# Block kernel (window attention, then FFT filter and convolution), last strips: VectorE's order written out by the plan, the last 1x1 convolution of an older strip between a strip's two transforms, and GpSimd's first tap as a product of its own

## The chip, the cores and the metric

One core of one Trainium2 chip. The metric is the device time of one execution in microseconds, the median of several runs. The core has five engines with queues of their own, each in order: TensorE (PE; its weight loads are shown as PEld), VectorE (DVE), ScalarE (ACT), GpSimd (POOL) and SyncE (SP), which here issues DMAs.

## The reference

Two layers over x of shape (8, 384, 64, 64) in float32. Layer 0 is a window attention. Layer 1, the one that the change touches, is, cut to what matters:

```python
def _L1_conv_ref(x, fft_filter, w_in, w_dw, w_out):
    t = jnp.einsum('bchw,oc->bohw', x, w_in)              # 1x1 convolution in
    tp = t.reshape(b, hid, hb, P, wb, P)                  # 8x8 blocks
    tf = jnp.fft.rfft2(tp, axes=(3, 5))
    tf = tf * fft_filter[None, :, None, :, None, :]
    t = jnp.fft.irfft2(tf, s=(P, P), axes=(3, 5)).reshape(b, hid, h, w)
    t = jax.lax.conv_general_dilated(t, w_dw, ...)        # 3x3, each channel by itself
    x1, x2 = (t[:, :hid // 2], t[:, hid // 2:])
    g = jax.nn.gelu(x1, approximate=False) * x2
    return jnp.einsum('bchw,oc->bohw', g, w_out)          # 1x1 convolution out

x = x + _L0_conv_ref(_gn(x), ...)
x = x + _L1_conv_ref(_gn(x), ...)
```

`_gn` normalises each group of 12 channels over a whole image, so layer 1 of an image starts only when layer 0 of that image is complete.

## The kernel before

An image is 8 strips of 8 rows (512 positions), 384 channels in three planes of 128 partitions. (b,s) stands for strip s of image b below. Layer 1 of image b runs beside layer 0 of image b+1; behind the last image's layer 0 there is only its own layer 1, strip after strip. All instructions are put out by a plan: `at(place, piece, ...)` notes a piece with a place, a number in which one unit is half a strip, and the pieces are traced in the order of their places. TensorE's matmuls are pinned to that order (`keep_in_program_order`, called `in_order` too). On the other engines a scheduler orders the instructions at build time by its own estimate of when each is ready, with the plan's order as priority; a pinned instruction stays behind the one traced before it on its engine.

The pieces of a strip (b,s) of layer 1, with u = 16 (b+1) + 2 + 2 s, and the names by which the profile knows their tiles:

- `load` "mix" at u-0.84 (x_mix, on SP); `normal_x1` (xn, ScalarE, L652); `mix` four times from u+0.28 (pt on TensorE, copied by ScalarE to t1, L662).
- `transform` j = 0, 1 at u+0.995 and u+1.02: the forward transform pf on TensorE, and VectorE's product with the filter (t2, L679, two for each j; the profile calls the tiles t).
- `back` at u+1.99: the inverse transform pz on TensorE, then ScalarE's copies into z (L707), a plane of 10 x 66 with a border. `borders` copies the third plane and then the border rows between a strip and the one above it: L716 writes the lower border of the strip above, L717 the upper border of this one.
- the 3x3 convolution, nine taps for each of the planes m = 0, 2, 1 in the order of `TAPS`: the centre tap 0 by ScalarE (L777), the others by VectorE (`conv`, L783, a multiply-add). Taps 6, 7, 8 read the lower border row and need the next strip's pz.
- for the strips in `on_pool`, (6,7) and (7,0) to (7,6), plane 1 is done elsewhere (`pool_taps`): ScalarE multiplies a tap (L751, pairs of tiles in three buffers), GpSimd adds (L755 for taps 0 and 1 together, L759 for each other one). Their planes 0 and 2 add up in PSUM (tile acc); other strips add up in SBUF (tile zz).
- for (7,7), in `on_pe`, all of plane 1 and five taps of plane 2 are matmuls (`conv_taps`, pc).
- `gate` at u+4.5: gelu on ScalarE (L798 or L801, L802), two products of half height on VectorE (L803, L804), and the product of planes 0 and 1 (L805), on GpSimd for strips in `on_pool`.
- `load` "finish" at u+5.16, and `finish` at u+6.10: the convolution out, pw on TensorE (from g1 first, then from the product g0), the additions to x_finish on VectorE (L833, L835 or L839), the output DMA on SP.

A strip's `finish` therefore comes, two strips on, behind that strip's `back` and before the next one's `mix`. The tiles pt, pf, pw and pz share four buffers of PSUM (tag "gemm"); acc and pc share two pairs of banks (tag "att").

Of the kernel before, what the change touches and what calls it, by code (L numbers as in the profile page):

```python
# [12 lines left out]
P = 128  # L13
# [24 lines left out]
def block_kernel(ctx: ExitStack, tc: tile.TileContext, out, x, consts, fsel, wqk, wv, bqk, bv,  # L38
# [262 lines left out]
    def at(place, piece, *args):  # L301
        plan.append((place, len(plan), piece, args))
# [362 lines left out]
    def transform(b, s, j):  # L665

        pf_ = [psum(f"pf_{b}_{s}_{j}_{p}") for p in range(2)]
        t2 = zs[b, s, "t2", j] = sb.tile([P, 2, 2, C // 2], F32, tag="t2", bufs=3, name=f"t2_{b}_{s}_{j}")  # L670
        for i in range(2):
            t1 = zs.pop((b, s, "t1", 2 * j + i))
            for h in range(2):
                for p in ((0, 1), (1, 0))[h]:
                    rows, cols = slice(p * 64, (p + 1) * 64), slice(h * 64, (h + 1) * 64)
                    matmul(pf_[p][cols, i * 192:(i + 1) * 192], fwd[rows, rows],
                           t1[rows, h * 192:(h + 1) * 192], start=True, stop=True)
        for p in range(2):
            nc.vector.tensor_tensor(t2[:, p], pf_[p][:, 0:C].rearrange("p (i c) -> p i c", i=2),  # L679
                                    feff.unsqueeze(1).to_broadcast([P, 2, C // 2]), ALU.mult)  # L680

    def back(b, s):

# [34 lines left out]

    TAPS = (4, 0, 1, 2, 3, 5, 6, 7, 8)
    on_pe = {(B - 1, NS - 1): {2: 5, 1: 9}}
    on_pool = [(B - 2, NS - 1)] + [(B - 1, s) for s in range(NS - 1)]

    def tap_matrices():
# [16 lines left out]
    def pool_taps(b, s, taps):  # L742

        z = zs[b, s, 1]
        for j in range(0, len(taps), 2):
            tag = ("o", "e", "eT")[zs["pairs"] % 3]
            zs["pairs"] += 1
            pair = sb.tile([P, 2, ST], F32, tag=tag, bufs=1, name=f"tap_{b}_{s}_{taps[j]}")
            for i, tap in enumerate(taps[j:j + 2]):
                dy, dx = TAPS[tap] // 3, TAPS[tap] % 3  # L750
                nc.scalar.activation(pair[:, i].rearrange("p (r c) -> p r c", c=SW), z[:, dy:dy + 8, dx:dx + SW],  # L751
                                     AF.Copy, scale=dw_sb[:, 1, TAPS[tap]:TAPS[tap] + 1])
            if tap == 1:
                zz = zs[b, s, "zz", 1] = row512("qk", 5, f"zz_{b}_{s}_1")
                nc.gpsimd.tensor_tensor(zz, pair[:, 0], pair[:, 1], ALU.add)  # L755
            else:
                zz = zs[b, s, "zz", 1]
                for i in range(len(taps[j:j + 2])):
                    nc.gpsimd.tensor_tensor(zz, zz, pair[:, i], ALU.add)  # L759

    def conv(b, s, m, tap):

        if m == 1 and (b, s) in on_pool:
            return
        z = zs[b, s, m]
        n = on_pe.get((b, s), {}).get(m, 0)
        if tap < max(n, 1):
            return
        if tap == max(n, 1):
            if (b, s) in on_pool:  # L770
                if m == 0:
                    zs[b, s, "in psum"] = psum2(f"acc_{b}_{s}")
                zz = zs[b, s, "in psum"][:, m // 2]
            else:
                zz = row512("zz", 5, f"zz_{b}_{s}_{m}")
            if n == 0:
                after_out(nc.scalar.activation(zz.rearrange("p (r c) -> p r c", c=SW), z[:, 1:9, 1:SW + 1],  # L777
                                               AF.Copy, scale=dw_sb[:, m, 4:5]))
                zs[b, s, "zz", m] = zz
            zs[b, s, "acc", m] = zz  # L780
        acc, old = zs[b, s, "acc", m], zs[b, s, "zz", m]
        dy, dx = TAPS[tap] // 3, TAPS[tap] % 3
        i = nc.vector.scalar_tensor_tensor(acc.rearrange("p (r c) -> p r c", c=SW),  # L783
                                           z[:, dy:dy + 8, dx:dx + SW], dw_sb[:, m, TAPS[tap]:TAPS[tap] + 1],
                                           old.rearrange("p (r c) -> p r c", c=SW), ALU.mult, ALU.add)

        if b < B - 1 and m and tap == 1:
            tc.keep_in_program_order(i)
        if b < B - 1:
            after_softmax(i)  # L790
        zs[b, s, "zz", m] = acc

    def gate(b, s):
        zz = {m: zs[b, s, "zz", m] for m in range(KC)}
        g1 = row512("g1", 2, f"g1_{b}_{s}")
        if (b, s) in on_pool:
            whole = row512("zz", 5, f"zz_{b}_{s}_0")
            nc.scalar.activation(whole, zz[0], AF.Gelu)  # L798
            zz[0] = whole
        else:  # L800
            nc.scalar.activation(zz[0], zz[0], AF.Gelu)  # L801
        nc.scalar.activation(g1[64:P], zz[2][0:64], AF.Gelu)  # L802
        nc.vector.tensor_tensor(g1[0:64], g1[64:P], zz[2][64:P], ALU.mult)  # L803
        nc.vector.tensor_tensor(g1[64:P], g1[64:P], zz[2][64:P], ALU.mult)  # L804
        (nc.gpsimd if (b, s) in on_pool else nc.vector).tensor_tensor(zz[0], zz[0], zz[1], ALU.mult)  # L805
        zs[b, s, "g"] = zz[0], g1

    def finish(b, s):


        g0, g1 = zs[b, s, "g"]
        t = xs[b, s, "finish"]

        full, lo, hi = slice(0, ST), slice(0, 256), slice(256, ST)
        pw = [psum(f"pw_{b}_{s}_{m}") for m in range(3 if (b, s) in on_pool else 2)]
        if (b, s) in on_pool:
            pw = [(p, m, full) for m, p in enumerate(pw)]
        else:
            pw2 = psum2(f"pw2_{b}_{s}")
            pw = [(pw[0], 0, full), (pw[1], 1, full), (pw2[:, 0, lo], 2, lo), (pw2[:, 1, lo], 2, hi)]  # L820

        for i, half, r in ((0, 0, 0), (1, 1, 1), (0, 1, 0), (1, 0, 1), (2, 0, 0), (3, 1, 1), (2, 1, 0), (3, 0, 1)):
            if i < len(pw) and not (len(pw) == 3 and i == 2):
                p, m, tok = pw[i]
                rows, cols = slice(r * 64, (r + 1) * 64), slice(half * 64, (half + 1) * 64)
                matmul(p[cols], wo_sb[rows, 1, m * P + half * 64:m * P + half * 64 + 64], g1[rows, tok],
                       start=True, stop=False)
        if len(pw) == 3:
            matmul(pw[2][0], wo_sb[0:64, 1, 2 * P:3 * P], g1[0:64], start=True, stop=False)
        for p, m, tok in pw:  # L830
            matmul(p, wo_sb[:, 0, m * P:(m + 1) * P], g0[:, tok], start=False, stop=True)
        for m in range(2):
            nc.vector.tensor_tensor(t[:, m, :], pw[m][0], t[:, m, :], ALU.add)  # L833
        if len(pw) == 3:
            nc.vector.tensor_tensor(t[:, 2, :], pw[2][0], t[:, 2, :], ALU.add)  # L835
            nc.sync.dma_start(out=rows_of(out[b], s), in_=t)
            return
        by_half = t[:, 2, :].rearrange("p (o n) -> p o n", o=2)
        zs["added"] = nc.vector.tensor_tensor(by_half, pw2[:, :, lo], by_half, ALU.add)  # L839
        nc.sync.dma_start(out=rows_of(out[b], s), in_=t)  # L840


# [3 lines left out]
    for b in range(B):  # L846
# [73 lines left out]
        for s in range(NS):  # L920
            u = first + 2 + 2 * s
            at(u - 0.84, load, b, s, "mix")
            at(u + 0.02, normal_x1, b, s)
            for i in range(4):
                at(u + (0.28, 0.45, 0.60, 0.78)[i], mix, b, s, i)
            for j in range(2):
                at(u + (0.995, 1.02)[j], transform, b, s, j)
            if b < B - 1:
                at(u + 1.985, small_tiles, u + 2)
            at(u + 1.99, back, b, s)  # L930
            at(u + 2.08 if b < B - 1 or s < NS - 1 else u + 1.991, borders, b, s)

            for n, m in enumerate((0, 2, 1)):
                for tap in range(1, 6):
                    at(u + (2.62, 3.10, 3.5)[n] + 0.05 * tap + (0.4 if n == 2 and tap > 3 else 0), conv, b, s, m, tap)
                for tap in range(6, 9):
                    at(u + 4.2 + 0.25 * (n * 3 + tap - 6) / 9, conv, b, s, m, tap)
            if (b, s) in on_pool:
                for place, taps in ((2.45, (0, 1)), (2.8, (2, 3)), (3.15, (4, 5)), (4.15, (6, 7)), (4.3, (8,))):
                    at(u + place, pool_taps, b, s, taps)  # L940
            if (b, s) in on_pe:
                at(u + 2.3, conv_taps, b, s)
            at(u + 5.16, load, b, s, "finish")
            at(u + 4.5, gate, b, s)
            at(u + 6.10, finish, b, s)

# [130 lines left out]
```

## Time and profile before

| | us |
|---|---|
| runs | 3560.96, 3565.46, 3568.88; median 3565.46 |
| the profiled execution | 3566.98, its span 3565.2, mean granted TensorE clock 0.99 |
| busy: TensorE, VectorE, ScalarE, GpSimd | 3472.5, 3048.4, 2519.4, 1047.6 |
| image 7's layer 1 in the span | from 3370.8 (its first xn) to 3565.2 |

The last image's strips in the timeline (us from the span's start):

| strip | mix pt starts | first filter product t starts |
|---|---|---|
| (7,1) | 3398.53 | 3408.57 |
| (7,2) | 3416.66 | 3427.59 |
| (7,3) | 3437.15 | 3447.35 |
| (7,4) | 3457.24 | 3467.32 |
| (7,5) | 3477.48 | 3487.30 |
| (7,6) | 3497.60 | 3507.07 |
| (7,7) | 3515.82 | 3526.38 |

How to read it: a line of the timeline has the start, the length of the merged run of like instructions, the engine, the line of the code, the operation, the tiles written and read (buffer numbers left out), shapes, the number of instructions, and in brackets the engine's idle time before it and what ended it. A line of the windows has, for PE, PEld, DVE, ACT and POOL, the busy time and the number of instructions, then the granted TensorE clock as a share of full speed, and the DMA share and rate.

### The profile page before, as it was taken

What the parts mean: (1) busy time and instruction counts of PE and PEld (TensorE: products, weight loads), DVE (VectorE), ACT (ScalarE), POOL (GpSimd) and SP (SyncE); (2) the same over time, 40 slices, a digit from 0 to 9 for tenths busy, and PEclk for the clock granted to TensorE, in tenths of its full rate; (3) what the DMA queues carried; (4) which work ended last, traced back from release to release, by engine and by line L of the source; (5) the groups of instructions that cost most, each with busy time, mean ns of one, the idle gap of its engine ahead of it and who ended that gap; (6) DMA issues with size and microseconds to landing.
All of it is one profiled execution on the core that took longest, in us unless ns stands there. A gap on an engine that the chain in (4) does not pass through costs nothing.

```text
span 3565.2 us, 93610 instructions
## 1 busy us (share of the span) xinstructions
PE 3472.5 (97%) x36454; PEld 2203.4 (62%) x36454; DVE 3048.4 (86%) x4330; ACT 2519.4 (71%) x4055; POOL 1047.6 (29%) x1688
## 2 busy tenths in 40 slices
PE   7999999999999999999999999999999999999988
PEld 5666666656666666666666666666566666666554
DVE  5766589889988899988998989988899888987987
ACT  4777677768777687776777767777777767776564
POOL 5333222223232233222323223223223222222244
PEclk8999999999999999999999999999999999999999
DMA  4333334334433244323433333423243333322432
GB/s 125 113 125 110 102 113 138 100 106 148 137 110 124 95 141 148 119 98 137 138 124 116 133 106 126 150 97 131 101 149 126 123 106 104 119 97 91 172 115 81
DMA packets 177255, 427.45 MB, mean 120 GB/s; under 512 B 26784, under 2 KB 29371, under 8 KB 176840
## 3 DMA queue, kind: packets, MB, share of 16 engines
q1 hardware_dynamic: 139984, 370.54, 29.8%
q0 software_dynamic: 36416, 50.65, 5.1%
q8 instruction: 317, 5.19, 0.6%
q14 instruction: 98, 0.80, 0.1%
q10 hardware_dynamic: 440, 0.27, 0.0%
HBM read 270.21 MB, written 100.79 MB: 104 GB/s over the span
## 4 chain that ended last, share of the span: by engine, by line
PE 88%; DVE 6%; ACT 3%; DMA 1%; issue 1%; POOL 1%; SPq 0%; ACTq 0%; POOLq 0%; DVEq 0%
PE pq L61 26%; PE pr L61 14%; PE pvv L61 13%; PE pt L61 11%; PE pw L61 6%; PE pA L61 4%; PE pz L61 4%; PE pS L61 3%; PE pT L71 3%; PE pf L61 2%; DVE zz L783 2%; PE ln L61 1%; DVE acc L783 1%; ACT tap L751 1%; DVE e L535 1%
## 5 line engine op out<-in xcount | busy, mean ns | idle before, releaser
L783 DVE SCALAR_TENSOR_TENSOR zz<-z,dw_sb,zz 128x512 f32<-128x512 f32 x1331 | 1021.0, 793 | 10.9
L61 PE MATMUL pq<-y,wqk_sb 128*128 128x512 f32 x2160 | 997.8, 599 | 0.8 <-DVE y L436 0.8
L613 POOL DMA_DIRECT2D oT<-o x960 | 480.4, 508 | 981.8 <-ACT z L716 443.4
L61 PEld LDWEIGHTS pq<-y,wqk_sb 128*128 128x128 f32 x2160 | 400.8, 190 | 457.3 <-issue 413.6
L61 PE MATMUL pt<-wi_sb,xn 128*128 128x384 f32 x1536 | 537.7, 489 | 9.4 <-ACT kcd L468 4.9
L61 PE MATMUL pr<-oT,wp_sb 128*128 128x512 f32 x1152 | 522.6, 593 | 0.0
L61 PE MATMUL pvv<-wv_sb,y 128*128 128x192 f32 x2880 | 509.7, 327 | 0.0
L61 PEld LDWEIGHTS pvv<-wv_sb,y 128*128 128x128 f32 x2880 | 472.1, 191 | 47.6 <-issue 32.8
L61 PEld LDWEIGHTS pt<-wi_sb,xn 128*128 128x128 f32 x1536 | 291.6, 191 | 238.2 <-issue 77.2
L450 POOL COPY y<-y 128x384 f32<-128x384 f32 x112 | 84.7, 756 | 1138.1 <-PE pvv L61 665.9
L61 PEld LDWEIGHTS pr<-oT,wp_sb 128*128 128x128 f32 x1152 | 219.1, 190 | 268.1 <-issue 251.4
L468 ACT ACTIVATE kcd<-pq,bqk_sb 32x512 f32<-32x512 f32 x512 | 348.4, 680 | 9.1
L468 ACT ACTIVATE qab<-pq,bq_sb,cst 96x512 f32<-96x512 f32 (+1 forms) x256 | 197.6, 772 | 198.6 <-PE pq L61 195.4
L501 ACT COPY v<-pvv 128x384 f32<-128x384 f32 x256 | 121.6, 475 | 208.6 <-PE pvv L61 207.5
L468 ACT ACTIVATE kab<-pq,bqk_sb 96x512 f32<-96x512 f32 (+1 forms) x256 | 174.1, 680 | 95.8 <-PE pq L61 91.4
L468 ACT ACTIVATE qcd<-pq,bq_sb,cst 96x512 f32<-96x512 f32 (+1 forms) x256 | 197.5, 772 | 36.0 <-PE pq L61 29.3
L528 DVE TENSOR_TENSOR e<-pS,bias 128x512 f32<-128x512 f32 (+2 forms) x200 | 108.3, 548 | 113.6 <-PE pS L61 113.6
L380 POOL TENSOR_TENSOR sq<-sq 128x512 f32<-128x512 f32 x122 | 202.7, 1661 | 5.8
L535 DVE TENSOR_TENSOR e<-e,mx 128x1024 f32<-128x1024 f32 x128 | 196.9, 1538 | 4.1
L61 PE MATMUL pw<-zz,wo_sb 128*128 128x512 f32 x496 | 182.2, 510 | 0.0
L545 DVE TENSOR_REDUCE rc<-e 128x16 f32<-128x1024 f32 x128 | 155.1, 1212 | 29.5 <-ACT e L540 29.4
L623 DVE SCALAR_TENSOR_TENSOR x_add<-pr,vec,x_add 128x512 f32<-128x512 f32 x192 | 142.9, 744 | 36.4 <-PE pr L61 35.6
(162 smaller groups left out, 5365.1 us busy)
## 6 DMA issues: line engine op xcount, KB each, us to landing
x_add<-in_x_dram SPq DMA_DIRECT2D x64, 768.0 KB, 9.7
x1d<-x_add SPq DMA_DIRECT2D x64, 768.0 KB, 3.7
x_mix<-x1d SPq DMA_DIRECT2D x64, 768.0 KB, 4.2
x_finish<-x1d SPq DMA_DIRECT2D x64, 768.0 KB, 6.9
out_dram<-x_finish SPq DMA_DIRECT2D x64, 768.0 KB, 4.2
x_norm<-in_x_dram SPq DMA_DIRECT2D x61, 768.0 KB, 8.2
x_stats<-in_x_dram SPq DMA_DIRECT2D x56, 768.0 KB, 7.5
oT<-o POOLq DMA_DIRECT2D x192, 96.0 KB, 3.8
```

The source lines that it names most:

```text
L61: tc.keep_in_program_order(nc.tensor.matmul(*args, **kw))
L71: tc.keep_in_program_order(nc.tensor.transpose(*args, **kw))
L380: nc.gpsimd.tensor_tensor(sq[:, 0, :], sq[:, 0, :], sq[:, k, :], ALU.add)
L450: nc.gpsimd.tensor_copy(dst[:, :, :, :, 0:4], src[:, :, :, :, 4:8])
L468: return nc.scalar.activation(dst[to:to + n], pq[of:of + n], AF.Identity, bias=bias[of:of + n], scale=scale)
L501: nc.scalar.copy(v[:, 384 * g:384 * (g + 1)], pvv[:, 0:384])
L528: nc.vector.tensor_tensor(e5[:, odd, :, a:z, :], pS[:, odd, :, a:z, :], bias_t[br, kind, odd].unsqueeze(2).to_broadcast([P, 2, z - a, 64]) ...
L535: zs["soft"] = nc.vector.tensor_tensor(e, e, mx.unsqueeze(2).to_broadcast([P, 2 * NS, 64]), ALU.subtract)
L545: nc.vector.tensor_reduce(rc, e, AX.X, ALU.add)
L613: nc.gpsimd.dma_start(out=oT[to % P:to % P + z - a, to // P, rows], in_=o[row + a:row + z, h // 2, of:of + n])
L623: after_softmax(nc.vector.scalar_tensor_tensor(t[:, m, :], pr, bp_sb[:, m:m + 1], t[:, m, :], ALU.add, ALU.add))
L783: i = nc.vector.scalar_tensor_tensor(acc.rearrange("p (r c) -> p r c", c=SW), z[:, dy:dy + 8, dx:dx + SW], dw_sb[:, m, TAPS[tap]:TAPS[tap] ...
```

## The change

`last_strips` is (6,7) and all of image 7. For them VectorE's filter products, taps, gate products and final additions are pinned in the plan's order (`in_plan`), and places change: `borders` at u+1.991; taps 1 to 5 of plane 0 at u+2.30, tap 1 of plane 2 at u+3.10 and its taps 2 to 5 at u+3.60, taps 6 to 8 of plane 2 at u+4.10 and of plane 0 at u+4.11; for (7,7) plane 0 at u+2.40 and plane 2 at u+2.50; the load for `finish` at u+4.16 and `finish` at u+5.5, that is two strips on between that strip's `transform` and `back`. (6,7)'s taps are no longer held behind the softmax. In `pool_taps` tap 0 is a GpSimd multiplication from z itself at u+2.30, the pairs are (1,2), (3,4), (5), (6,7), (8), and each tap is added by itself. The diff, whole but for its context lines:

```diff
@@ -676,8 +676,8 @@
-            nc.vector.tensor_tensor(t2[:, p], pf_[p][:, 0:C].rearrange("p (i c) -> p i c", i=2),
-                                    feff.unsqueeze(1).to_broadcast([P, 2, C // 2]), ALU.mult)
+            in_plan(b, s, nc.vector.tensor_tensor(t2[:, p], pf_[p][:, 0:C].rearrange("p (i c) -> p i c", i=2),
+                                                  feff.unsqueeze(1).to_broadcast([P, 2, C // 2]), ALU.mult))
 ...
@@ -718,8 +718,13 @@
+    def in_plan(b, s, i):
+        if (b, s) in last_strips:
+            in_order(i)
 ...
+    last_strips = [(B - 2, NS - 1)] + [(B - 1, s) for s in range(NS)]
 ...
@@ -742,21 +747,21 @@
-        for j in range(0, len(taps), 2):
-            tag = ("o", "e", "eT")[zs["pairs"] % 3]
-            zs["pairs"] += 1
-            pair = sb.tile([P, 2, ST], F32, tag=tag, bufs=1, name=f"tap_{b}_{s}_{taps[j]}")
-            for i, tap in enumerate(taps[j:j + 2]):
-                dy, dx = TAPS[tap] // 3, TAPS[tap] % 3
-                nc.scalar.activation(pair[:, i].rearrange("p (r c) -> p r c", c=SW), z[:, dy:dy + 8, dx:dx + SW],
-                                     AF.Copy, scale=dw_sb[:, 1, TAPS[tap]:TAPS[tap] + 1])
-            if tap == 1:
-                zz = zs[b, s, "zz", 1] = row512("qk", 5, f"zz_{b}_{s}_1")
-                nc.gpsimd.tensor_tensor(zz, pair[:, 0], pair[:, 1], ALU.add)
-            else:
-                zz = zs[b, s, "zz", 1]
-                for i in range(len(taps[j:j + 2])):
-                    nc.gpsimd.tensor_tensor(zz, zz, pair[:, i], ALU.add)
+        if taps[0] == 0:
+            zz = zs[b, s, "zz", 1] = row512("qk", 5, f"zz_{b}_{s}_1")
+            nc.gpsimd.tensor_scalar(zz.rearrange("p (r c) -> p r c", c=SW), z[:, 1:9, 1:SW + 1],
+                                    dw_sb[:, 1, 4:5], None, ALU.mult)
+            return
+        tag = ("o", "e", "eT")[zs["pairs"] % 3]
+        zs["pairs"] += 1
+        pair = sb.tile([P, 2, ST], F32, tag=tag, bufs=1, name=f"tap_{b}_{s}_{taps[0]}")
+        for i, tap in enumerate(taps):
+            dy, dx = TAPS[tap] // 3, TAPS[tap] % 3
+            nc.scalar.activation(pair[:, i].rearrange("p (r c) -> p r c", c=SW), z[:, dy:dy + 8, dx:dx + SW],
+                                 AF.Copy, scale=dw_sb[:, 1, TAPS[tap]:TAPS[tap] + 1])
+        zz = zs[b, s, "zz", 1]
+        for i in range(len(taps)):
+            nc.gpsimd.tensor_tensor(zz, zz, pair[:, i], ALU.add)
 ...
@@ -784,9 +789,10 @@
-        if b < B - 1 and m and tap == 1:
+        in_plan(b, s, i)
+        if b < B - 1 and m and tap == 1 and (b, s) not in last_strips:
 ...
-        if b < B - 1:
+        if b < B - 1 and (b, s) not in last_strips:
 ...
@@ -800,9 +806,12 @@
-        nc.vector.tensor_tensor(g1[0:64], g1[64:P], zz[2][64:P], ALU.mult)
-        nc.vector.tensor_tensor(g1[64:P], g1[64:P], zz[2][64:P], ALU.mult)
-        (nc.gpsimd if (b, s) in on_pool else nc.vector).tensor_tensor(zz[0], zz[0], zz[1], ALU.mult)
+        in_plan(b, s, nc.vector.tensor_tensor(g1[0:64], g1[64:P], zz[2][64:P], ALU.mult))
+        in_plan(b, s, nc.vector.tensor_tensor(g1[64:P], g1[64:P], zz[2][64:P], ALU.mult))
+        if (b, s) in on_pool:
+            nc.gpsimd.tensor_tensor(zz[0], zz[0], zz[1], ALU.mult)
+        else:
+            in_plan(b, s, nc.vector.tensor_tensor(zz[0], zz[0], zz[1], ALU.mult))
 ...
@@ -830,13 +839,14 @@
-            nc.vector.tensor_tensor(t[:, m, :], pw[m][0], t[:, m, :], ALU.add)
+            in_plan(b, s, nc.vector.tensor_tensor(t[:, m, :], pw[m][0], t[:, m, :], ALU.add))
 ...
-            nc.vector.tensor_tensor(t[:, 2, :], pw[2][0], t[:, 2, :], ALU.add)
+            in_plan(b, s, nc.vector.tensor_tensor(t[:, 2, :], pw[2][0], t[:, 2, :], ALU.add))
 ...
+        in_plan(b, s, zs["added"])
 ...
@@ -928,21 +938,29 @@
-            at(u + 2.08 if b < B - 1 or s < NS - 1 else u + 1.991, borders, b, s)
+            last = (b, s) in last_strips
+            at(u + (1.991 if last else 2.08), borders, b, s)
 ...
-                for tap in range(1, 6):
+                for tap in range(1, 9) if last else ():
+                    if (b, s) == last_strips[-1]:
+                        at(u + (2.40, 2.50, 2.45)[n], conv, b, s, m, tap)
+                    elif tap > 5:
+                        at(u + (4.11, 4.10, 0)[n], conv, b, s, m, tap)
+                    else:
+                        at(u + (2.30, 3.10 if tap == 1 else 3.60, 2.30)[n], conv, b, s, m, tap)
+                for tap in range(1, 6) if not last else ():
 ...
-                for tap in range(6, 9):
+                for tap in range(6, 9) if not last else ():
 ...
-                for place, taps in ((2.45, (0, 1)), (2.8, (2, 3)), (3.15, (4, 5)), (4.15, (6, 7)), (4.3, (8,))):
+                for place, taps in ((2.30, (0,)), (2.45, (1, 2)), (2.8, (3, 4)), (3.15, (5,)), (4.05, (6, 7)), (4.06, (8,))):
 ...
-            at(u + 5.16, load, b, s, "finish")
+            at(u + (4.16 if last else 5.16), load, b, s, "finish")
 ...
-            at(u + 6.10, finish, b, s)
+            at(u + (5.5 if last else 6.10), finish, b, s)
 ...
```

## The prediction

> **What bounds the kernel now.** I read the page's engine shares and slices first, then the chain of waits from 2900 us on, then the waits, the timeline and the clock of the tail. Writing (7,3) for strip 3 of image 7: the diff touches strips (6,7) and (7,0) to (7,7) alone, that is the last 240 us, where no attention work is left to fill an engine's gaps.
>
> ```profile
> PE 3472.5 (97%) x36454; PEld 2203.4 (62%) x36454; DVE 3048.4 (86%) x4330; ACT 2519.4 (71%) x4055; POOL 1047.6 (29%) x1688
> ...
> PE   7999999999999999999999999999999999999988
> ```
>
> TensorE bounds the whole, but its two slices that fall to 8 are the last two. So the tail is where time can be had. Of the waits between 3398 and 3516 us (engine, line, who it waited for, total, times, longest) these matter:
>
> ```profile
> POOL zz L759 <- ACT tap L751: 49.9, 6, 10.1
> PEld pz L61 <- DVE t L679: 15.4, 23, 2.5
> PE pz L61 <- DVE t L679: 9.4, 10, 2.2
> DVE acc L783 <- ACT z L716: 11.2, 5, 2.4
> ```
>
> GpSimd's 50 us cost nothing by themselves (it is off the path). TensorE waits for VectorE's filter product t (L679) before the inverse transform pz; VectorE then waits 2.4 us a strip for the row copy (L716) that follows pz. One strip's turn, (7,4), in the timeline (start, length, engine, line):
>
> ```profile
> 3464.16 3.13 DVE L783 SCALAR_TENSOR_TENSOR acc<-z,dw_sb,acc 128x512 f32<-128x512 f32 x4
> 3465.08 1.53 PE L61 MATMUL pf<-t,cst 64*64 64x192 f32 x32
> ...
> 3467.32 1.02 DVE L679 TENSOR_TENSOR t<-pf,feff 128x384 f32<-128x384 f32 x2
> ...
> 3467.94 1.15 PE L61 MATMUL pz<-cst,t 64*64 64x64 f32 x32 [1.33 <-DVE t L679]
> 3468.26 0.75 DVE L783 SCALAR_TENSOR_TENSOR acc<-z,dw_sb,acc 128x512 f32<-128x512 f32 x1
> ...
> 3468.92 1.02 DVE L679 TENSOR_TENSOR t<-pf,feff 128x384 f32<-128x384 f32 x2
> 3469.53 2.97 PE L61 MATMUL pz<-cst,t 64*64 64x64 f32 x62 [0.43 <-DVE t L679]
> ...
> 3472.28 3.69 DVE L783 SCALAR_TENSOR_TENSOR acc<-z,dw_sb,acc 128x512 f32<-128x512 f32 x5 [2.35 <-ACT z L716]
> ...
> 3474.80 2.84 PE L61 MATMUL pw<-zz,wo_sb 128*128 128x512 f32 x6
> ...
> 3475.40 3.98 POOL L759 TENSOR_TENSOR zz<-zz,tap 128x512 f32<-128x512 f32 x3 [8.12 <-ACT tap L751]
> ...
> 3479.35 1.28 POOL L755 TENSOR_TENSOR zz<-tap 128x512 f32<-128x512 f32 x1
> ...
> 3480.70 5.33 POOL L759 TENSOR_TENSOR zz<-zz,tap 128x512 f32<-128x512 f32 x4
> ...
> 3485.98 1.29 POOL L805 TENSOR_TENSOR zz<-zz,zz 128x512 f32<-128x512 f32 x1
> ```
>
> The forward transform pf ends at 3466.61, yet VectorE is in four taps until 3467.3, and puts a tap between the two pairs of t. TensorE stands still 1.33 and 0.43 us, and pz's last 62 instructions then take 2.97 us. The windows of one microsecond say why (busy time of PE, PEld, DVE, ACT, POOL, then the clock): after that gap the clock is halved, after (7,6)'s shorter one it isn't.
>
> ```profile
> 3470.00:3471.00 1.00, 1.00 (x30) 1.00 (x32) 0.00 (x0) 0.04 (x1) 0.00 (x0) 0.50 1.02 430
> ...
> 3510.00:3511.00 1.00, 1.00 (x53) 1.00 (x44) 0.00 (x0) 0.64 (x2) 0.00 (x0) 1.00 0.00 0
> ```
>
> The filter products of (7,1) to (7,7) start at 3408.57, 3427.59, 3447.35, 3467.32, 3487.30, 3507.07 and 3526.38: 117.8 us for six turns, 19.0 and 19.3 where the clock held, 19.8 to 20.0 where it fell. TensorE's work in one turn is 16.1: mix 7.84, pf 1.53, pz 2.0 (at full clock), the last convolution pw 2.08 + 2.68 (3511.06 to 3513.14 to 3515.82). VectorE's is 16.9: 16 taps at 0.72 (five take 3.51, eight 5.96), four t at 0.51, three additions at 0.6, two gate products at 0.69. Neither is full; they wait for each other in turn.
>
> **The change, part by part.** *pw moved.* The pw of the strip two back goes from behind pz to between pf and pz, with its three additions, its output DMA and, one place unit earlier, its x_finish load on SP. Instructions are the same, so TensorE's 16.1 stays; the load takes 6.9 us to land, has some 12 us until its use, and ahead of it on SP stand only a store and a load that are as early as now: 0. pw can't start at once: pt, pf, pw and pz share four banks, and pf holds all four until t has read them. What the move buys is that pz no longer waits for t, and VectorE has work (four taps of m=2) while pz and ScalarE make the border row; its 2.0 to 2.35 us wait there goes. A new wait comes: the additions (L833) now stand in VectorE's queue ahead of 15 taps, the gate products and the next t, so all these wait for pw.
>
> *VectorE's order fixed.* I add up the new turn from the start of t. First t 0.5 and 0.2 to TensorE; pw's first part 2.1; first full product 0.86; 0.3 to VectorE (its row at 3496.08 waits 0.35): 4.0. VectorE has only four t and one tap, 2.8, so it waits 1.2. Additions, at TensorE's pace 0.86 + 0.86 + 0.6: 6.3. Fifteen taps at 0.72: 17.1. The border row is there in time: pz ends at 4.0 - 0.3 + 1.7 + 2.1 = 7.5, the copies 1.4 later (as 3510.3 to 3511.7), 8.9, or 9.4 if the third plane's copy goes ahead of them as the plan now has it, against 6.3 + 2.9 = 9.2 where the first is needed: nothing. Two gate products at 0.72 pitch: **18.5**. With the taps at 0.69 (3.51 for five, less the last one's tail) it is 18.0, at 0.75 it is 19.0. Six turns: 111.0 against 117.8, **-6.8** (-9.8 to -3.8).
>
> *Clock.* TensorE now idles 18.5 - 16.1 = 2.4 us a turn, in one piece. The nearest rows: 1.33 + 0.43 (7,4) and 1.07 + 0.43 (7,5) halved it for some 3.4 us, 0.72 + 0.43 (7,6) didn't. Halved turns cost 0.7 more (20.0 against 19.3). Where the slow stretch lies on pz or pt it falls into TensorE's slack; on pw, VectorE waits. I take 0.5 a turn, **+3.0**; ends 0 and 1.7 (half of 3.4), so 0 and +10.
>
> The Trainium skill ("TensorE: Matmul & The Clock Gate", Part 1) speaks of a free-running window of about 3.4 us and of the slow clock after an idle one; here 1.5 us of idleness were enough, so the row decides. By the rule alone no turn would be slowed, and the sum would lack these 3.0.
>
> *GpSimd's first product.* Tap 0 leaves ScalarE (0.71 a strip, where it has room) and becomes a GpSimd multiplication; tap 1, so far added to it in one instruction, gets its own. So GpSimd runs nine plus the gate product instead of eight plus it. No row shows a multiplication by a column on it: between its copy of 384 elements at 0.756 us, or 1.0 for 512, and its product under contention, 1.66; I take 1.3, nearest to its additions (1.27). It needs only its own strip's pz and falls into the 8 us in which GpSimd waits: 0, as long as nothing on the path waits for GpSimd (first rival).
>
> *Head.* Between 3366 and 3387 the old strip (6,6) still has its sums in SBUF:
>
> ```profile
> 3381.18 4.92 POOL L759 TENSOR_TENSOR zz<-zz,tap 128x512 f32<-128x512 f32 x3 [2.76 <-ACT tap L751]
> ...
> 3381.64 1.65 DVE L803 TENSOR_TENSOR g<-g,zz 64x512 f32<-64x512 f32 x1
> ```
>
> Beside GpSimd three products take 1.65 each instead of 0.69. (6,7)'s first five taps now come ahead of them in the plan, which may carry them clear (-2.9), or one more GpSimd instruction may hold VectorE (+1.7). First t of (7,1): **0**, ends -3 and +2.
>
> The Trainium skill ("SBUF — State Buffer", on the shared port pair) has a VectorE instruction with two SBUF inputs and a GpSimd one exclude each other for a whole instruction. That speaks against the added multiplication, and for the last strip too; by it the head alone would lose the full multiplication. The rows show the pairing only as 1.65 against 0.69.
>
> *End.* From the last t to the last addition it was 3560.48 - 3526.38 = 34.1. New: additions done at 6.3, eighteen taps (four, six, and eight of (7,7), placed ahead of (7,6)'s gate) 19.3, gate 20.7, four taps 23.6. TensorE's own convolution pc starts at 8.2, ends at 20.3; pw of (7,6) runs from 20.8, its additions end at 26.4; two of (7,7)'s three gate products at 27.8, pw 27.9 + 2.1 + 2.6, 0.3 and 0.6: 33.5, -0.6. (7,7)'s sums lie in SBUF and now run beside (7,6)'s last GpSimd additions: 0 to two taps at 1.68, +0.8. Together **+0.2** (-0.6 to +1.4).
>
> Sum: -6.8 + 3.0 + 0 + 0.2 = -3.6 on the profiled execution's 3567.0 (its span 3565.2): 3563.4. The median shown is 1.5 lower, 3565.5, so 3561.9; I say **3561**.
>
> **The rivals.** *The product behind the taps (slower).* Only VectorE and TensorE are pinned; ScalarE's and GpSimd's queues are not. Above, L805 comes behind all of the next strip's taps 0 to 5, though the plan has it after the first pair. It costs nothing today since pw comes 8 us later. With pw ahead of pz this closes a loop: pz's end to GpSimd's start 2.95 (3432.5 to 3435.44), eight additions 10.6, product 1.4, three full products 2.6, pz 2.1: 19.6 a turn, and 20.9 if the multiplication stands in it too; TensorE then idles 3.5 us and pw and pz run in the slow clock, up to 1.5. Six turns of 19.6 to 22.4: -0.2 to +17; 3573 in the middle. It decides once L805 starts later than some 22 us after pf's end. For it: the order of all six turns above. Against: the taps' places are closer to the plan's gate now, and with the plan's order (five additions ahead) the loop is 16.
>
> *The clock falls on pw every time.* 18.5 + 1.7 = 20.2, six turns 121.2, +3.4: 3569. For it: the gap lies directly ahead of pw. Against: in the turns shown half of each slow stretch lay on other work.
>
> *A bigger gain.* No halved clock, taps at 0.69, head -3: -9.8 - 3 + 0.2: 3553. For it: VectorE never again cuts into t, and the waits in the taps' way are gone.
>
> *It doesn't do what it says* is unlikely for VectorE and TensorE, whose order is pinned; for GpSimd it is the first rival.
>
> **How the numbers follow.** What a measurement can tell from no change is about 0.2%, 7 us: faster lies under 3558.3, slower over 3572.6. Forecast 0.46 (its own range 3554 to 3567; 0.19 of it faster, 0.27 same). Product behind the taps 0.27 (0.24 slower, 0.03 same). Clock on pw 0.10 (0.06 same, 0.04 slower). Bigger gain 0.17 (faster). Faster 0.36, same 0.36, slower 0.28. The range, 3549 to 3577, reaches over most of the bigger gain and half of the slow rival.
>
> **What would show it.** In the new timeline: pw between pf and pz; t four in a row, starts 18 to 19 us apart; VectorE's wait before L833 about 1.2 us, before the taps 6 to 8 nearly none; L805 ending before pw's full products; clock windows of 0.50 on pz or pt. I'd be wrong if TensorE waits at pw for L805, if VectorE waits over 2 us for L833, or if the first t of (7,1) moves by over 3 us.

## The result, and the profile after

The changed kernel takes **3584.06 us** (median of 4 runs, 3581.32 to 3589.29) against 3564.92 us for the kernel before on the same chip: ratio **1.0056** (95% interval 1.0043 to 1.0069), some 19 us slower. The forecast was 3561, the range ended at 3577. The profiled execution took 3589.29 us, its span 3587.3 (before 3565.2).

The page after, engine shares, TensorE's slices and its clock's slices:

```profile
PE 3496.4 (97%) x36454; PEld 2198.6 (61%) x36454; DVE 3051.5 (85%) x4330; ACT 2514.5 (70%) x4047; POOL 1059.7 (30%) x1696
...
PE   7999999999999999999999999999999999999888
...
PEclk8999999999999999999999999999999999999988
```

The same 36454 matmuls take 24 us more of TensorE's time (before 3472.5), while DVE's busy time hardly moves: not more work, but work at a lower clock. Three slices of TensorE fall to 8 instead of two, and the clock's last two fall with them. All of it is in the tail: ahead of (7,0)'s first pt TensorE is busy 3304.7 us before and 3304.9 after, from there on 167.7 and 191.5.

The mix (pt) of (7,1) to (7,7) starts at 3391.40, 3413.44, 3437.62, 3457.49, 3481.85, 3501.72 and 3526.12: turns of 22.0, 24.2, 19.9, 24.4, 19.9, 24.4, together 134.7 us against 117.3 before. Four of the six are long, the first two in a row and then every other one. The waits after, between 3398 and 3516 us (engine, line, whom it waited for, total, times, longest; the additions are now L842 and L844, GpSimd's multiplication L752):

```profile
POOL zz L752 <- ACT z L707: 51.1, 5, 15.9
...
DVE x_finish L842 <- PE pw L61: 18.9, 10, 4.5
...
PE pf L61 <- ACT t L662: 7.4, 10, 1.1
PE pw L61 <- DVE t L679: 6.2, 6, 2.1
...
ACT tap L760 <- POOL zz L764: 5.5, 5, 1.1
DVE x_finish L844 <- PE pw L61: 3.3, 5, 1.0
```

TensorE's waits for t before pz are gone, and so is VectorE's wait for the border row: both as foreseen. In their place VectorE waits for pw, up to 4.5 us at a time, and TensorE waits twice ahead of pw: for ScalarE's copies of pt (L662), then for t. Two turns in the timeline, the first at full clock, the second not:

```profile
3445.55 0.88 PE L61 MATMUL pf<-t,cst 64*64 64x192 f32 x16
...
3446.86 0.54 PE L61 MATMUL pf<-t,cst 64*64 64x192 f32 x2 [0.42 <-ACT t L662]
...
3448.46 0.88 PE L61 MATMUL pf<-t,cst 64*64 64x192 f32 x14 [1.06 <-ACT t L662]
...
3449.56 1.95 DVE L679 TENSOR_TENSOR t<-pf,feff 128x384 f32<-128x384 f32 x4
...
3450.18 2.60 PE L61 MATMUL pw<-g,wo_sb 64*64 64x512 f32 x10 [0.84 <-DVE t L679]
3451.43 0.74 DVE L788 SCALAR_TENSOR_TENSOR acc<-z,dw_sb,acc 128x512 f32<-128x512 f32 x1
3452.70 2.84 PE L61 MATMUL pw<-zz,wo_sb 128*128 128x512 f32 x6
3453.87 0.69 DVE L842 TENSOR_TENSOR x_finish<-pw,x_finish 128x512 f32<-128x512 f32 x1 [1.69 <-PE pw L61]
...
3456.19 11.76 DVE L788 SCALAR_TENSOR_TENSOR acc<-z,dw_sb,acc 128x512 f32<-128x512 f32 x15
...
3464.35 0.72 ACT L760 ACTIVATE tap<-z,dw_sb 128x512 f32<-128x512 f32 x1 [1.11 <-POOL zz L764]
...
3468.20 1.28 POOL L812 TENSOR_TENSOR zz<-zz,zz 128x512 f32<-128x512 f32 x1
...
3469.43 1.95 DVE L679 TENSOR_TENSOR t<-pf,feff 128x384 f32<-128x384 f32 x4
...
3470.05 4.44 PE L61 MATMUL pw<-g,wo_sb 64*64 64x512 f32 x10 [0.84 <-DVE t L679]
3471.30 0.74 DVE L788 SCALAR_TENSOR_TENSOR acc<-z,dw_sb,acc 128x512 f32<-128x512 f32 x1
3474.42 5.49 PE L61 MATMUL pw<-zz,wo_sb 128*128 128x512 f32 x6
3476.53 0.69 DVE L842 TENSOR_TENSOR x_finish<-pw,x_finish 128x512 f32<-128x512 f32 x1 [4.48 <-PE pw L61]
```

TensorE's idle stretch ahead of pw is the same in both: 0.42 + 1.06 + 0.84 = 2.3 us. But the second pw takes 4.44 + 5.49 instead of 2.60 + 2.84, 4.5 us more, and VectorE, which has one tap between t and the additions, hands all of it on. The windows of the second turn (busy time of PE, PEld, DVE, ACT, POOL, then the clock):

```profile
3469.00:3470.00 1.00, 0.20 (x6) 0.00 (x0) 0.97 (x3) 1.00 (x3) 1.00 (x2) 0.79 0.00 0
...
3475.00:3476.00 1.00, 1.00 (x2) 0.34 (x1) 0.00 (x0) 0.00 (x0) 0.00 (x0) 0.50 0.08 31
3479.00:3480.00 1.00, 1.00 (x10) 0.17 (x12) 0.06 (x1) 0.00 (x0) 0.00 (x0) 0.59 0.00 0
```

The clock is halved at 3469.6 and comes back at 3479.8, just as pw ends: 10.2 us of half clock, and pw is all that TensorE computes in them.

### The profile page after: what moved, and what is told of

It reads as the page before. It is cut to its first block, busy times and chain, and to the rows that moved or that the text cites. A ratio compares the mean times of both kernels' runs of the same rounds, so it can differ in the third digit from the quotient of the medians.

```text
span 3587.3 us, 93605 instructions
## 1 busy us (share of the span) xinstructions
PE 3496.4 (97%) x36454; PEld 2198.6 (61%) x36454; DVE 3051.5 (85%) x4330; ACT 2514.5 (70%) x4047; POOL 1059.7 (30%) x1696
## 4 chain that ended last, share of the span: by engine, by line
PE 88%; DVE 7%; ACT 2%; DMA 2%; issue 1%; POOL 0%; SPq 0%; ACTq 0%; DVEq 0%; POOLq 0%
PE pq L61 26%; PE pr L61 14%; PE pvv L61 13%; PE pt L61 11%; PE pw L61 8%; PE pA L61 3%; PE pS L61 3%; PE pz L61 3%; PE pT L71 3%; PE pf L61 2%; DVE acc L788 2%; DVE zz L788 2%; PE ln L61 1%; DVE e L535 0%; DMA x_stats<-in_x_dram 0%
## 5 line engine op out<-in xcount | busy, mean ns | idle before, releaser
L61 PE MATMUL pw<-zz,wo_sb 128*128 128x512 f32 x496 | 199.3, 547 | 0.0
L707 ACT ACTIVATE z<-pz 128x512 f32<-128x512 f32 x192 | 111.9, 655 | 90.8 <-PE pz L61 90.8
```

What stands on the lines that cost most here:

```text
L61: tc.keep_in_program_order(nc.tensor.matmul(*args, **kw))
L707: nc.scalar.activation(z[:, 1:9, 1:SW + 1].rearrange("p r (w c) -> p w r c", c=WS), by_window(zs[b, s, "pz"][m]), AF.Copy)
```

## The experiments

The theory after this result: the moved pw stands directly behind TensorE's idle stretch and so is what runs in the slow clock; the fixed order of VectorE is no loss by itself. Rivals: the fixed order costs the time (VectorE can't take another tap while it waits), or GpSimd's longer chain does. "Turn" in the table is the mean of the six from (7,1) to (7,7) by the starts of pt in the profile; each ratio is against the kernel before on the same chip.

| run | us | ratio to before (95%) | turn |
|---|---|---|---|
| before | 3564.6 to 3566.6 | 1 | 19.5 |
| the change | 3584.1 | 1.0056 (1.0043 to 1.0069) | 22.5 |
| e1 without the move | 3549.5 | 0.9953 (0.9935 to 0.9970) | 17.9 |
| e2 without the fixed order | 3571.9 | 1.0019 (1.0009 to 1.0028) | 20.2 |
| e3 without GpSimd's product | 3588.3 | 1.0061 (1.0042 to 1.0080) | 21.5 |
| e4 forward transform twice | 3566.9 | 1.0001 (0.9988 to 1.0013) | 19.7 |
| e5 five pair buffers | 3581.5 | 1.0048 (1.0031 to 1.0065) | 22.4 |
| e6 alternating taps | 3608.1 | 1.0115 (1.0097 to 1.0133) | 25.1 |
| e7 as e1, alternating | 3568.3 | 1.0009 (1.0000 to 1.0018) | 20.4 |
| e8 as e4, alternating | 3596.4 | 1.0087 (1.0069 to 1.0106) | 23.7 |
| e9 three taps before the additions | 3564.0 | 1.0003 (0.9994 to 1.0013) | 19.8 |
| e10 e9 and five buffers | 3565.4 | 0.9996 (0.9983 to 1.0010) | 19.5 |
| e11 as e1, alternating across strips | 3571.0 | 1.0010 (0.9997 to 1.0024) | 20.8 |
| e12 e10, alternating across strips | 3585.9 | 1.0066 (1.0046 to 1.0086) | 22.4 |
| e13 the fixed order alone | 3551.9 | 0.9965 (0.9951 to 0.9978) | 17.9 |

**One part undone at a time.** e1 puts `finish` back behind pz and its load back to its old time:

```diff
-            at(u + (4.16 if last else 5.16), load, b, s, "finish")
+            at(u + 5.16, load, b, s, "finish")
-            at(u + (5.5 if last else 6.10), finish, b, s)
+            at(u + (6.105 if last else 6.10), finish, b, s)
```

> The changed kernel with the last convolution and its load put back to their old places (behind the inverse transform, the additions between the taps 6 to 8 of plane 2 and of plane 0); the pinned order and GpSimd's own product stay. Theory (the loss is pw standing directly behind TensorE's gap, where it runs at half clock for 10 us every other turn, with VectorE's queue held behind its additions): VectorE's turn becomes 2.0 + 16 x 0.786 + 1.9 + 1.4 = 17.9 us and some waits, so 18 to 19 us against 19.6 before: 3552 to 3566. Rival (the fixed order of the taps is the loss by itself, 0.786 us a tap against 0.69): no better than 3575.

Theory confirmed, and by more than it asked: e1 beats the kernel before by 17 us. One of its turns of 17.56 us in the timeline:

```profile
3474.52 1.95 DVE L679 TENSOR_TENSOR t<-pf,feff 128x384 f32<-128x384 f32 x4
3475.14 2.89 PE L61 MATMUL pz<-cst,t 64*64 64x64 f32 x96
3476.39 6.35 DVE L788 SCALAR_TENSOR_TENSOR acc<-z,dw_sb,acc 128x512 f32<-128x512 f32 x8
...
3479.93 2.84 PE L61 MATMUL pw<-zz,wo_sb 128*128 128x512 f32 x6
...
3482.65 1.28 DVE L842 TENSOR_TENSOR x_finish<-pw,x_finish 128x512 f32<-128x512 f32 x2
3483.85 0.68 DVE L844 TENSOR_TENSOR x_finish<-pw,x_finish 128x512 f32<-128x512 f32 x1
3484.45 6.15 DVE L788 SCALAR_TENSOR_TENSOR acc<-z,dw_sb,acc 128x512 f32<-128x512 f32 x8
```

No wait of VectorE or TensorE in these lines: eight taps lie between t and the additions, pz and pw run while they do, and the engines meet only at t. In the whole turn TensorE has one marked wait, 0.16 us for a copy of pt. e2 takes `in_order` out of `in_plan`, e3 puts the old `pool_taps` and its old first places back:

```diff
     def in_plan(b, s, i):
-        if (b, s) in last_strips:
-            in_order(i)
+        return
```

> The changed kernel with VectorE's order left to the scheduler; the move and GpSimd's own product stay. Theory (half clock on pw): the gap before pw stays, and so does most of the loss: 3573 to 3590. Rival (the fixed order is the loss): back to 3560 to 3568.

> The changed kernel with GpSimd's taps as they were before (taps 0 and 1 both from ScalarE, added in one instruction); the move and the pinned order stay. Theory: GpSimd is off the path, 3578 to 3590, the same as the changed kernel. Rival (ScalarE's copies t1 come late because its taps wait for GpSimd, which has one instruction more): one GpSimd instruction less brings the copies 1.3 us forward, the gap before pw falls under 1.5 us, the clock stays: 3568 to 3575.

e3 is as the theory has it: GpSimd's product has no part in the loss. e2 falls between the two forecasts: the scheduler then puts three taps ahead of the additions, and VectorE's wait for pw there is 0.61 to 0.74 us:

```profile
3465.79 2.33 DVE L787 SCALAR_TENSOR_TENSOR acc<-z,dw_sb,acc 128x512 f32<-128x512 f32 x3
3468.74 0.69 DVE L841 TENSOR_TENSOR x_finish<-pw,x_finish 128x512 f32<-128x512 f32 x1 [0.61 <-PE pw L61]
```

The slow clock still comes, for 3.4 us a time. So with the move the free order is better than the fixed one. e13 asks for the fixed order as the only part (e1's edit and e3's together):

> VectorE's fixed order (with its places) as the only part of the change: the output convolution in its old place, GpSimd's first sum as in the kernel before. Theory (the fixed order is a gain by itself, GpSimd's own product does nothing in either place, and the move alone turns the whole into a loss): turns of 17.5 to 17.7 us, 3546 to 3553 us, ratio 0.9935 to 0.9970 as with the product. Rival (the product is needed: without it GpSimd starts only after two of ScalarE's taps and is late for the output products of the old place too): turns above 18 us, 3555 us or more.

0.9965: the fixed order alone is the gain, 14 us, and GpSimd's product adds nothing that can be told (the two intervals overlap). "The fixed order" here is the order with its new places in the plan; no run had the places without it and without the move, so the two aren't told apart. The version to keep is the fixed order with the output convolution in its old place, e1 or e13: faster than both kernels.

**The clock by itself.** e4 leaves every order as in the change, and only has TensorE compute image 7's forward transform twice, into the same place:

```diff
-        for i in range(2):
-            t1 = zs.pop((b, s, "t1", 2 * j + i))
+        for i, again in ((0, 0), (0, 1), (1, 0), (1, 1)):
+            if again and b < B - 1:
+                continue
+            t1 = zs[b, s, "t1", 2 * j + i]
 ...
+                    if again:
+                        in_order(nc.tensor.matmul(*args, start=True, stop=True))
 ...
```

> The changed kernel with each matmul of the forward transform of image 7 done twice, the second time with the same result in the same place: 32 more matmuls of 64x192 a strip, 1.5 us of TensorE, which fall into its gaps while it waits for t1 and for VectorE's t. Nothing else changes. Theory (the clock): TensorE's clock stays at 1.00 over pw, the turns of 24.3 us fall to some 20 us; three of them and the end, 13 to 17 us: 3567 to 3572. Rival (VectorE's order or ScalarE's late copies are the loss, the clock a companion): no gain, or a loss of up to 1.5 us a strip: 3583 to 3596.

More work, and 17 us less than the change. Its turn:

```profile
3463.78 0.39 PE L61 MATMUL pf<-t,cst 64*64 64x192 f32 x3 [1.05 <-ACT t L662]
...
3465.51 2.60 PE L61 MATMUL pw<-g,wo_sb 64*64 64x512 f32 x10 [0.20 <-DVE t L685]
...
3468.04 2.84 PE L61 MATMUL pw<-zz,wo_sb 128*128 128x512 f32 x6
3469.20 0.69 DVE L848 TENSOR_TENSOR x_finish<-pw,x_finish 128x512 f32<-128x512 f32 x1 [1.69 <-PE pw L61]
```

The doubled products fill 1.1 of the 2.3 idle us; the clock stays at 1.00 in every turn, pw takes 2.60 + 2.84, and each turn from (7,2) on is 19.87, the length of the change's turns at full clock ((7,1)'s is 18.75). VectorE's wait is the same 1.69. Each beside the kernel before on its own chip, e4 loses 0.3 us and the change 19.1. So the half clock is nearly all of the 19 us. Only the end still has it, for 6.8 us from 3548.0 on. The rest of the way to e1, another 17, goes with turns of 19.87 instead of 17.56 at full clock, and VectorE's waits for pw, 1.69 + 0.17 + 0.17 a turn, are nearly all of that difference.

**Where the idle stretch comes from.** e5 gives GpSimd's pairs five buffers, so that ScalarE's tap (L760) needn't wait 1.11 us ahead of the copies:

```diff
-        tag = ("o", "e", "eT")[zs["pairs"] % 3]
+        tag = ("o", "e", "eT", "sq", "oT")[zs["pairs"] % 5]
-        pair = sb.tile([P, 2, ST], F32, tag=tag, bufs=1, name=f"tap_{b}_{s}_{taps[0]}")
+        pair = sb.tile([P, 2, ST], F32, tag=tag, bufs=2 if tag == "oT" else 1, name=f"tap_{b}_{s}_{taps[0]}")
```

> The changed kernel with five buffers for GpSimd's tap pairs instead of three. Theory (the half clock is set off by TensorE's idle stretch of 2.3 us ahead of the output products, of which 1.1 us are the copies of the transform's input that stand in ScalarE's queue behind a tap that waits 1.1 us for a pair buffer): that wait is gone, the copies come about 1 us sooner, the idle stretch falls to 1.2 to 1.6 us, about what the run with the doubled transform left; the clock holds at 1.00 through the output products in most turns, turns are 19 to 20 us, and the time falls to 3562 to 3570 us. Rival (the copies are late behind the GELUs and the other taps in any case, the buffer is not what holds them): idle stretch above 2 us, turns still alternate between 19.9 and 24.3, 3580 to 3588 us.

Refuted in its number: no gain that can be told (3581.5, the rival's range). The copies do come earlier, but the stretch only changes its owner:

```profile
3466.82 0.87 PE L61 MATMUL pf<-t,cst 64*64 64x192 f32 x14 [0.92 <-ACT t L662]
3469.34 3.43 PE L61 MATMUL pw<-g,wo_sb 64*64 64x512 f32 x10 [1.64 <-DVE t L679]
```

0.92 + 1.64 is 2.6 us. The copies were not the last in line; behind them VectorE's queue was just as late with t. e9 goes at that queue: two of the fifteen taps behind the additions go ahead of them.

```diff
-                        at(u + (2.30, 3.10 if tap == 1 else 3.60, 2.30)[n], conv, b, s, m, tap)
+                        at(u + (2.30, 3.10 if tap <= 3 else 3.60, 2.30)[n], conv, b, s, m, tap)
```

> The changed kernel with three taps of the third plane, instead of one, between VectorE's t and the additions; the output convolution stays between the two transforms. Theory (the additions stand behind only one tap, so VectorE waits 1.7 us for TensorE even at full clock, all behind them comes late by that, t too, and TensorE's idle stretch ahead of the output products is what VectorE's queue lacks): VectorE's wait falls to about 0.1 us; what is left of TensorE's idle stretch are the copies in ScalarE's queue, about 1.5 us; if the clock holds by that, turns of 18.5 to 19.6 us without alternation and 3556 to 3566 us; if not, the slow turns stay and 3574 to 3582. Rival (the clock falls on the output products wherever VectorE's additions stand): turns still alternate, 3580 to 3588 us.

> As the run with three taps, and five pair buffers for GpSimd besides, so that ScalarE's copies come earlier too: in the run with five buffers alone TensorE's wait for the copies fell from 1.5 to 0.9 us, but its wait for VectorE's t rose by as much. Theory (both causes of the idle stretch have to go together; either alone leaves the other as the last one): idle stretch of 1.0 to 1.5 us, clock 1.00 through the output products in all turns, turns of 18.2 to 18.8 us, 3553 to 3560 us, 25 to 30 below the changed kernel. Rival (no such pairing: the two edits bring nothing beyond three taps alone): within 3 us of the run before it in this batch.

e9 takes 20 us off the change, all that it had lost. Its turn of 18.64 us:

```profile
3457.28 0.87 PE L61 MATMUL pf<-t,cst 64*64 64x192 f32 x14 [0.50 <-ACT t L662]
...
3458.98 2.60 PE L61 MATMUL pw<-g,wo_sb 64*64 64x512 f32 x10 [0.83 <-DVE t L679]
3460.23 2.33 DVE L788 SCALAR_TENSOR_TENSOR acc<-z,dw_sb,acc 128x512 f32<-128x512 f32 x3
3461.51 2.84 PE L61 MATMUL pw<-zz,wo_sb 128*128 128x512 f32 x6
3462.67 0.69 DVE L842 TENSOR_TENSOR x_finish<-pw,x_finish 128x512 f32<-128x512 f32 x1
```

VectorE's wait of 1.69 is gone, t comes earlier, and TensorE idles 0.50 + 0.83 = 1.3 us instead of 2.3. (A wait of 0.46 for the border row is back, which the change didn't have.) Two of the tail's turns still have the slow clock (from 3401 and from 3497 us, 6.8 us each). e10 is no different from e9 (the intervals overlap): its idle stretches are the same 0.51 + 0.82, so the buffers aren't what is left, and the expected pairing of two causes isn't there.

**Taps alternating (e6, e7, e8, e11, e12): a miss.** In the pinned order two taps in a row stand 0.79 us apart; I took that for the price of writing the same plane, and let the planes alternate (e6, e7, e8: places in steps of 0.001), then the strips. The second, as in e11 and without its lines for the old place of the convolution:

```diff
-                        at(u + (4.11, 4.10, 0)[n], conv, b, s, m, tap)
+                        at(u + 4.293 + 0.002 * tap - (0, 0.006, 0)[n], conv, b, s, m, tap)
-                        at(u + (2.30, 3.10 if tap == 1 else 3.60, 2.30)[n], conv, b, s, m, tap)
+                        at(u + (2.298 + 0.002 * tap, 3.10 if tap == 1 else 3.60, 2.30)[n], conv, b, s, m, tap)
```

> The changed kernel with VectorE's taps of the two planes taken alternately instead of plane after plane. Theory (two taps in a row into the same plane cost 0.786 us of queue each, alternating ones about 0.69, and VectorE's product t comes late by that): fourteen taps ahead of t take about 10 us instead of 11, TensorE's wait of 0.8 us for t goes, its idle stretch ahead of the output products falls from 2.3 to about 1.5 us; the clock may hold, then 3560 to 3570 us; if it still drops every other turn, about 1 us a turn is left, 3574 to 3579 us. Rival (the pitch of 0.786 is not that of the same plane but of the pinned queue or of the port that VectorE and GpSimd share): no difference, 3582 to 3588 us and pitch 0.78.

> Output convolution back in its old place (as in the first experiment), VectorE's order still fixed, taps of the two planes alternating. The first experiment's turn of 17.56 us has VectorE busy 16.93 and TensorE 17.11 us. Theory (VectorE's queue sets that turn, 16 taps at 0.78): turn falls to TensorE's own 17.1 us, 3 to 4 us less over seven turns, 3545 to 3548 us against a kernel before of 3565 to 3567, ratio 0.9940 to 0.9950. Rival (TensorE sets the turn already, or alternating does nothing): 3549 to 3551 us, turn 17.5.

> The changed kernel with image 7's first transform computed twice (the same products into the same place, so more work on TensorE in each turn, outputs unchanged) and alternating taps: it asks whether the moved output convolution can pay when the clock holds. Theory (VectorE's queue sets the turn of 19.87 us of the doubled kernel; t comes 0.8 us late): turns 18.9 to 19.2 us, 3559 to 3563 us, still above the 17.56 us a turn of the old place. Rival (TensorE's 18.6 us and its wait for the copies set the turn): 19.7 to 19.9 us, 3566 to 3568 us.

> Output convolution in its old place, VectorE's order fixed, and the new strip's first five taps alternating with the older strip's last ones, so that neighbours write different accumulator tiles. In the trace of the alternating run before, two taps in a row into the same tile (two planes of one strip share one) stood 0.79 apart, into different tiles 0.66. Theory: some nine of sixteen taps a turn gain 0.12 us, VectorE's queue falls from 16.9 to about 15.9 us, TensorE's 17.1 us sets the turn: 17.2 instead of 17.56, 3546 to 3548 us (ratio 0.9940 to 0.9950). Rival (the pitch hangs on something else, or an accumulator's first product comes late): 3549 to 3553, turn 17.5 or more.

> Moved output convolution with all three: three taps ahead of the additions, five pair buffers, and taps alternating between two strips. It asks whether the moved place can come up to the old one. Theory (VectorE's queue 1 us shorter still, but TensorE's loop through its own work, pf and the copies is now the longest): turns 17.6 to 18.6 us at clock 1.00, 3549 to 3557 us, no better than the output convolution in its old place. Rival (moved place pays once the queues are in order): below 3546 us.

All five are slower than the same kernel without it. Alternating the planes of one strip (e6) left the pitch at 0.79, and VectorE waited besides for the third plane's first product (L782), which now stood behind the GELUs in ScalarE's queue. Alternating two strips (e11) did bring the pitch to 0.66, but the older strip's last taps then came later, and the GELU and the gate products with them. The timeline of e11:

```profile
3459.64 7.33 DVE L788 SCALAR_TENSOR_TENSOR acc<-z,dw_sb,acc 128x512 f32<-128x512 f32 x11
3469.01 0.69 DVE L809 TENSOR_TENSOR g<-g,acc 64x512 f32<-64x512 f32 x1 [2.04 <-ACT g L808]
```

The 1.2 us that eleven taps saved (7.33 against 8.54 in e9) became a wait of 2.04. TensorE then waits 2.87 us for t ahead of pz, and the clock falls once in every turn: seven falls, from 3409.7 on, each 20.48 us after the last. A shorter queue in the wrong order is worth nothing here, since a pinned queue stands still wherever its next instruction isn't ready.

## Why the prediction was wrong

**The step that failed** is the clock: "I take 0.5 a turn, +3.0". The length of the idle stretch was foreseen, "2.4 us a turn, in one piece"; it is 2.3, in three pieces, and 1.5 of it is a wait for ScalarE's copies of pt, which the sum didn't have. But the price came from turns in which half of a slow stretch of 3.4 us lay in TensorE's slack. Behind the move there is no slack: pw is directly behind the stretch, VectorE's pinned queue is directly behind pw, and the slow clock stayed for two or three times as long. A slow turn costs 24.4 - 19.87 = 4.5 us, over two and a half times my upper bound of 1.7. Six turns at 19.87 would be 119.2; measured are 134.7: **+15.5** where the sum had +3.0. e4 says the same from the other side: with the clock held its six turns take 118.1.

**The turn, 18.5.** At full clock it is 19.87, above the bound of 19.0. The first addition starts 4.31 after t (4.0 by my sum) and the taps behind the third start at 6.63 (6.3): +0.3. Fifteen taps take 11.80 to the next instruction, 0.786 each and not 0.72: +1.0. My 0.72 came from rows in which steps of 0.79 and of 0.66 stand side by side, which I read as the free scheduler changing between accumulator tiles. (VectorE's work in a turn, "16.9", adds up to 16.7 by its own terms; nothing was worked out from it.) So even with the clock held the six turns would have been 119.2 against 117.3: **in this form the move could not gain in its turns at full clock either**, and e4's 118.1 agrees (its ratio is 1.0001). VectorE's wait of 1.2, for which I had the right place, is 1.69 and was the key: with four t and one tap to cover pw, the pinned queue pays it each turn, while the old place covers pw with eight taps.

**What I credited to the move belonged to the fixed order.** I wrote that what the move buys is that pz no longer waits for t and the taps no longer for the border row. In e1 and e13 pw is in its old place and both waits are gone too: t comes as soon as pf ends since no tap is put in its way. The prediction added the three parts up in one turn and never asked what each would do alone.

**The end, +0.2 (-0.6 to +1.4).** From the first t of (7,7), 3538.02, to the end of the last addition, 3582.63, it is 44.6 us against 34.1: +10.5. Both older strips' pw run at half clock there (4.44 + 5.35 and 4.80 + 5.49, so 4.4 and 4.9 above 5.44). The same missed price, which is most of it.

**Head, 0 (-3 to +2).** From pt of (7,0) to pt of (7,1) 23.2 us instead of 26.9: the three gate products of (6,6) take 0.69 each, clear of GpSimd, which is 2.9 of it. That is 3.7 better. By the mark of the forecast, the first t of (7,1), it is 34.0 instead of 36.9 us behind pt of (7,0): 2.9 better, at the good end. (Read from the span's start that t moves by 6.4, of which 3.5 are the tail's earlier start.)

**GpSimd's product, 0.** Right: it takes 1.56 us (taken 1.3, within the bounds), in its own idle time; e3 and e13 show no difference. **The first rival** didn't come: L812 starts at 3468.20, before pw, in the plan's order. **The second rival**, the clock on pw, was the right mechanism, with 10% and a price of 1.7 us that let it end at 3569. It came in four turns of six rather than in each, at up to 4.5.

In the pair of profiles: head -3.7, turns +17.4, end +11.8 (from pt of (7,7) to the end of the span, 49.4 to 61.2) make 25.5; the spans differ by 22.1, since pt of (7,0) started 3.5 earlier in this execution. That start lies anywhere from 3365.5 to 3374.3 in the fifteen traces.

## What to carry to other kernels

In this kernel an idle stretch of TensorE was paid by what stood right behind it. Ahead of moving work there, ask who waits for that work at half speed, and how much its waiter has to do meanwhile: here one tap, 0.74 us, against a pw of 5.4 or 9.9. And price the parts of a change one by one: a fixed order that gains 14 us and a move that loses 35 looked, as a sum, like nothing.

## What the runs showed of the hardware

**The clock moves on a grid.** In the trace after, from (7,1) on, it falls at 3404.7, 3425.2, 3469.6, 3514.0, 3537.9 and 3565.1 us; the distances from the third are 19.0, 13.0, 13.0, 20.0 and 28.0 times 3.413 us. A turn of 19.87 is 5.8 such windows, one of 24.4 is 7.1, and the two together are 13.0: from the second on, each slow turn meets the grid where the one before it did. So the same stretch is split differently in the two kinds of turn. In the window that ended at 3469.58 TensorE idled 0.42 + 1.06 + 0.38 = 1.9 us, and the clock fell; in the one that ended at 3449.10 it was 0.42 + 1.06 = 1.5, the rest fell into the next, and it held.

But idle time in one window isn't the whole rule. Four windows, with their length, TensorE's busy time, its matmuls, the clock, DMA share and rate: two of the trace after, one of e3, one of e10:

```profile
3445.69:3449.10 3.41, 1.92 (x32) 1.00 0.02 7
3534.43:3537.85 3.42, 1.92 (x31) 1.00 0.00 0
3448.00:3451.42 3.42, 1.77 (x22) 1.00 0.00 0
3445.14:3448.56 3.42, 2.09 (x33) 1.00 0.00 0
```

The clock held behind the first and the third, and fell behind the second and the fourth, the busiest of all. What else counts no run here settles.

**The way back.** Behind a fall in the trace after the clock stayed low for two windows (once) or three. The three from 3469.58 on, with the time that pw's first part (the matmuls from g1) takes in each:

```profile
3469.58:3472.99 3.41, 2.94 (x9) 0.50 0.15 31
3472.99:3476.41 3.42, 1.50 (x2) 0.50 0.52 199
3476.41:3479.82 3.41, 0.00 (x0) 0.50 0.02 5
```

TensorE is busy throughout the second, and the clock still stayed low behind it; it came back behind the third, which held only pw's second part. All six falls went like this: the clock stayed low behind each window with 1.2 us or more of the first part, and came back behind the first window without it. That the first part is the cause isn't shown: in e2 a slow window with 3.11 us of it and the last 0.6 of pf brought the clock back (3421.70 to 3425.11). In the kernel before, where the slow window lay on pz and the beginning of pw, it came back after one, in all five falls from (7,2) on.

The Trainium skill ("TensorE: Matmul & The Clock Gate", Part 1) has this window, 3413 ns and free-running, and the grid agrees. It gives at least one idle window as the condition of the fall; here 1.9 idle us of 3.41, and less, were enough. It gives at least one busy window as that of the return; here one that was busy throughout (3472.99 to 3476.41) was not enough.

**VectorE's pitch hangs on the accumulator's tile.** A tap (128x512) lasts 0.75 us in either case; the next one starts 0.79 after it if both write the same tile (the change), another plane of it included (e6), and 0.66 if they write different ones (e11, all eleven of the taps shown). Whether this is the chip or a wait that the program puts between them was not tried.
